# Unread products in TensorE's waits, counts taken out of a comparison, and another order of the first stages: a two-layer graph network on one core

## Chip, cores and metric

One core of a Trainium2 chip. The metric is the device time of one execution in microseconds (us). A core has five engines with a queue each: TensorE (PE: matrix products; PEld is its weight load), VectorE (DVE), ScalarE (ACT), GpSimd (POOL) and SyncE (SP, which here issues nearly all DMA transfers). A queue runs in order; engines wait for each other through semaphores.

## What is computed

There are 128 graphs of 128 nodes with 512 features. Both layers work on each graph alone:

```python
def hypergraph_conv(x, adj, W, b):
    H = (adj != 0).astype(x.dtype)
    w = adj.reshape(N, -1)[:, :C]                 # first row of adj
    xw = jnp.einsum('ncd,hd->nch', x, W)
    Dn = jnp.einsum('nce,ne->nc', H, w)
    Dn = jnp.where(Dn > 0, 1.0 / Dn, 0.0)
    Be = H.sum(axis=1)
    Be = jnp.where(Be > 0, 1.0 / Be, 0.0)
    m = Be[:, :, None] * jnp.einsum('nce,nch->neh', H, xw)
    out = Dn[:, :, None] * jnp.einsum('nce,neh->nch', H, m)
    return out + b
# layer 0
h = jnp.maximum(_layernorm(x), 0.0)
x0 = h
h = jax.nn.relu(hypergraph_conv(h, adj, W1, b1))  # 512 -> 1024
h = layer_norm(h, gamma, beta)
x = x + hypergraph_conv(h, adj, W2, b2) + x0      # 1024 -> 512
# layer 1
h = jnp.maximum(_layernorm(x), 0.0)
agg = (adj @ h) / jnp.maximum(adj.sum(-1), EPS)
x = x + jax.nn.relu(jnp.concatenate([h, agg], -1) @ W.T)
```

`Be` is one over the number of nodes in each hyperedge: the counts of the change.

## The kernel before

One graph fills the 128 partitions. A graph g passes through some sixty small stages (each a Python function that issues a few instructions), and five graphs are in flight. `step(s)` writes out by hand in which order the stages of graphs s-4 to s+2 are issued; there is a `head()` for the start, 131 calls of `step` (the stages that `head` or an index rule out are skipped), and a `tail()` for the last five graphs, called a to e (123 to 127). Nothing is reordered afterwards: the order of the calls is the order of each engine's queue, and semaphores are placed by data.

Weight products are split into high, low and difference parts: `product` (L376) runs the h and the l part of each into one bank of PSUM (rm, gm, bm, am by layer), and the d part into another (rd, gd, bd, ad), as fp32r products of 512 columns, four at a time: 0.9 us for four. Plain fp32 products are ps_s (L305, incidence matrix), pz (L343, features times node matrix), py (L517) and pc (L185, the beta row). Every split costs work on three engines: ACT writes h (L126 for weights, L356, L466), VectorE or POOL the l part, VectorE the d part.

What graph g needs, in the names of the trace: x is loaded (`load_x`), `x_sums`, `x_spread`, `scales`, `x_norm` make h0; `load_adjb` brings adj in blocks; `incidence` (L286, seven VectorE instructions) transposes it, sets it to 0 and 1, counts, and makes sb; `node_matrix` multiplies to ps_s and ACT copies it to s; `node_scale` makes dinv; `conv1_nodes` makes pz, which `conv1_high/low/rest` split into z; `conv1_weights` is rm and rd; `conv1_main`, `conv1_out`, `conv1_bias` make r; `inner_sums`, `inner_spread`, `inner_norm` normalise it; `inner_out` sends it to DRAM and `inner_in` reads it back in blocks (nb), `inner_turn` transposes (nt), `inner_high/low/rest` split it into nh, nl, nd; `conv2_weights` is gm and gd; g gets a bias (`conv2_bias`, c0) and goes into py; `conv2_out` adds py to x; `layer1_*` do the same normalising and trip for the second layer (h, hb, ht, hh, hl, hd) with products bm, bd (mean part) and am, ad (self part); `mean_*` make the mean operator from adj (`mean_operator` is four VectorE instructions, `mean_out` and `mean_in` a trip through DRAM); `aggregate` (L599) joins both; `finish` stores.

In the head the weights also come in and are split: `w1[half]`, `w2[half]` and `w3[half]` have `high(i)` on ACT, `low(i)` and `rest(i)` on VectorE, each for half of the columns; `scale_w2(k)` multiplies the second weights by gamma in place after `beta_row(k)` has read them on TensorE.

SP issues in program order and a DMA waits there for its buffers: `load_adjb` has two (`adjb`, L214), freed by the transpose in `incidence`. PSUM has eight banks: six named "w" (`bank`, L82) and two named "n" (`small_bank`, L86) for ps_s, pz and py.

Of the kernel before, what the change touches and what calls it, by code (L numbers as in the profile page):

```python
# [24 lines left out]
def gnn_kernel(  # L25
# [31 lines left out]
    nc = tc.nc  # L57
# [17 lines left out]
    def combine(eng, dst, a, b, op):  # L75

        width = 256 if eng is nc.gpsimd else dst.shape[1]
        for c in range(0, dst.shape[1], width):
            s = slice(c, c + width)
            eng.tensor_tensor(dst[:, s], a[:, s], b[:, s], op)  # L80

    def bank(name):  # L82

        return psum.tile([P, 512], FP, tag="w", name=name)

    def small_bank(name):  # L86

        return psum.tile([P, 512], FP, tag="n", name=name, bufs=2)

    done = set()  # L90

# [193 lines left out]
    @stage  # L285
    def incidence(g):  # L286


        HT[g] = at = pool.tile([P, P], FP, tag="ht", name="adjt")
        nc.vector.transpose(at, ADJB.pop(g))  # L290
        SB[g] = sb = pool.tile([P, P + 1], FP, tag="sb", name="sb")
        nc.vector.tensor_scalar(sb[:, P : P + 1], at[:, 0:1], DOWN_12, None, MUL)
        nc.vector.tensor_scalar(at, at, 0.0, None, ALU.not_equal)
        cnt = pool.tile([P, 1], FP, tag="cnt", name="cnt", bufs=2)
        nc.vector.tensor_reduce(cnt, at, AX.X, ADD)

        nc.vector.tensor_scalar(cnt, cnt, 1.0, None, MAX)
        nc.vector.reciprocal(cnt, cnt)
        nc.vector.tensor_scalar(sb[:, :P], at, cnt, None, MUL)
# [26 lines left out]
    @stage  # L326
    def x_spread(g):
        spread((1, g), X[g], H0[g], D)
# [47 lines left out]
    def product(left, halves, main, name):  # L376
        kk = KD * len(halves)

        def right(m, k):
            return getattr(halves[k // KD], "hld"[m])[:, k % KD, :]  # L380

        pm, pd = bank(name + "m"), bank(name + "d")
        for i in range(2):
            for k in range(kk):
                nc.tensor.matmul(pm, left[i](k), right(i, k), start=(i == 0 and k == 0),  # L385
                                 stop=(i == 1 and k == kk - 1))
        main(pm)
        for k in range(kk):
            nc.tensor.matmul(pd, left[2](k), right(2, k), start=(k == 0),  # L389
                             stop=(k == kk - 1), skip_group_check=True)  # L390
        return pd
# [291 lines left out]
    def head():  # L683
        copy(eps_root, eps, AF.Sqrt)
        load_x(0)
        load_adjb(2)
        for half in range(2):
            for i in range(2):
                load_w1(half, i)
        load_affine()  # L690
        load_adjb(0, nc.scalar)
        load_x(1)
        load_adjb(1)
        x_sums(0)
        load_adj(0)
        x_spread(0)
        for half in range(2):
            load_w2(half)
        load_bias(b2_bc, b2)
        w1[0].high(0)  # L700
        scales(0, 1)
        x_norm(0)
        w1[0].high(1)
        incidence(0)
        load_x(2)
        w1[0].low(0)
        node_matrix(0)
        conv1_nodes(0)
        w1[0].low(1)
        w1[1].high(0)  # L710
        w1[0].rest(0)
        conv1_high(0)
        w1[1].high(1)
        load_bias(b1_bc, b1)
        conv1_low(0)
        conv1_rest(0)
        incidence(1)
        x_sums(1, "A")
        x_spread(1)
        node_scale(0)  # L720
        w1[0].rest(1)
        scales(1, 1)
        w1[1].low(1)
        x_norm(1)
        conv1_weights(0, 0)
        beta_row(0)
        scale_w2(0, nc.scalar)
        conv1_main(0, 0)
        beta_row(1)
        scale_w2(1, nc.scalar)  # L730
        w1[1].low(0)
        w1[1].rest(0)
        w1[1].rest(1)
        node_matrix(1)
        node_scale(1)
        conv1_nodes(1)
        conv1_high(1, True)
        conv1_weights(0, 1)
        conv1_low(1)
        conv1_rest(1)  # L740
        beta_row(2)
        beta_row(3)
        conv1_main(0, 1)
        conv1_weights(1, 0)
        conv1_out(0, 0)
        scale_w2(2, nc.vector)
        scale_w2(3, nc.vector)
        conv1_bias(0, 0, nc.vector)
        w2[0].high(0)
        w2[0].high(1)  # L750
        conv1_out(0, 1)
        conv1_bias(0, 1, nc.vector)
        beta_row(4)
        beta_row(5)
        load_adjb(3)
        load_w3(0)
        load_w3(1)
        beta_row(6)
        beta_row(7)
        inner_sums(0)  # L760
        conv1_weights(1, 1)
        inner_spread(0)
        w2[0].low(1)
        residual(0)
        scale_w2(4, nc.vector)
        scale_w2(5, nc.vector)
        scales(0, 2)
        inner_norm(0)
        scale_w2(6, nc.vector)
        scale_w2(7, nc.vector)  # L770
        w2[0].low(0)
        incidence(2)
        inner_out(0)
        x_sums(2)
        x_spread(2)
        scales(2, 1)
        w2[1].high(0)
        w2[1].low(0)
        x_norm(2)
        node_matrix(2)  # L780
        w2[1].high(1)
        node_scale(2)
        load_adjb(4)
        conv1_nodes(2)
        conv1_main(1, 0)
        conv1_main(1, 1)
        conv1_high(2)
        w2[0].rest(1)
        conv1_low(2)
        conv1_rest(2)  # L790
        beta_out()
        inner_in(0)
        load_x(3)
        inner_turn(0)
        residual(1)
        conv1_out(1, 0)
        w3[0].high(0)
        conv1_bias(1, 0, nc.vector)
        w2[1].low(1)
        load_x(4)  # L800
        inner_high(0)
        conv1_weights(2, 0)
        conv1_out(1, 1)
        conv1_bias(1, 1, nc.vector)
        conv1_weights(2, 1)
# [8 lines left out]
        load_adjb(5)  # L814
        inner_rest(0)
        w3[0].high(1)
        w2[1].rest(1)
        incidence(3)
        conv2_weights(0)
        x_sums(3)  # L820
        x_spread(3)
        node_matrix(3)
        scales(3, 1)
        x_norm(3)
        residual(2)
        node_scale(3)
        conv2_main(0)
        conv1_main(2, 0)
        conv2_weights_out(0)
        conv1_nodes(3)  # L830
        conv2_bias(0, nc.vector)
        conv2_nodes(0)
        conv1_high(3, True)
        conv1_main(2, 1)
        conv1_low(3)
# [12 lines left out]
        scales(0, 3)  # L848
        inner_low(1, nc.vector)
        inner_rest(1)  # L850
        layer1_norm(0)
        layer1_trip_out(0)
        w3[1].high(0)
        conv2_weights(1)
        inner_sums(2)
        inner_spread(2)
        w3[0].low(1)
        scales(2, 2)
        conv2_main(1)
        inner_norm(2)  # L860
        conv2_weights_out(1)
        mean_operator(0)
        conv2_bias(1, nc.vector)
        inner_out(2)
        conv2_nodes(1)
        conv1_weights(3, 1)
        w3[1].low(0)
        mean_out(0)
        w3[0].low(0)
        conv2_out(1)  # L870
        layer1_trip_in(0)
        w3[1].high(1)
        mean_in(0)
        load_adj(1)
        x_sums(4)
        residual(3)
        x_spread(4)
        scales(4, 1)
        x_norm(4)
        incidence(4)  # L880
        layer1_turn(0)
        w3[1].low(1)
        layer1_high(0)
        node_matrix(4)
        mean_transpose(0)
        node_scale(4)
        layer1_low(0, nc.vector)
        inner_in(2)
        w3[0].rest(1)
        w3[1].rest(1)  # L890
        w3[1].rest(0)
        w3[0].rest(0)
        load_x(5)
        layer1_rest(0)
        load_adjb(6)

    def tail():
# [58 lines left out]
        layer1_low(c)  # L956
        finish(b)
        mean_out(c)
        conv2_nodes(d)
        layer1_rest(c)  # L960
        mean_in(c)
# [30 lines left out]
        mean_in(d)  # L992
        conv2_bias(e)
        finish(c)
        conv2_nodes(e)
        conv2_out(e)
        layer1_high(d)
# [82 lines left out]
```

## Time and profile before

| | |
|---|---|
| Time, median of 7 runs | 2514.29 us (2513.45 to 2516.66) |
| The profiled execution: time, span | 2513.88 us, 2512.1 us |
| Granted TensorE clock, mean of the span | 0.995 |
| Busy: PE, DVE, ACT, POOL | 2469.0, 2121.7, 1976.2, 1739.9 us |
| One graph in the body | 19.05 us |
| First product after which TensorE has no gap | 98.7 us |

How to read the profile: a line of instructions gives line, engine, operation, the tile written and the tiles read, the shape, and the count; a bracket names how long the engine sat idle before and whose work ended the wait. A fp32 product appears as two records. "Clock" is the share of TensorE's full clock that was granted in that stretch; TensorE's ends are modelled, so a product's row may overlap the next. A stretch is given by its limits in us from the start of the span.

### The profile page before, as it was taken

The numbers are of one execution on the slowest core, as the hardware profiler recorded it, in microseconds if no ns is written. First come the engines' busy times: TensorE is split into PE (matmuls) and PEld (weight loads), VectorE is DVE, ScalarE is ACT, GpSimd is POOL, SyncE is SP. The second block draws the span as 40 slices with busy tenths as digits, with TensorE's granted clock in tenths as the row PEclk, the third lists the DMA queues.
The fourth block names the chain that finished last, engine by engine and source line by source line (L and its number), as shares of the span: only waits on it lengthen the run. The fifth ranks groups of instructions, "written<-read, shape, count | busy, mean of one in ns | idle before, by whom it ended". The sixth has DMA issues, their size and how long they took to land.

```text
span 2512.1 us, 41377 instructions
## 1 busy us (share of the span) xinstructions
PE 2469.0 (98%) x11152; PEld 2003.6 (80%) x11152; DVE 2121.7 (84%) x4907; ACT 1976.2 (79%) x4112; POOL 1739.9 (69%) x2290
## 2 busy tenths in 40 slices
PE   6899999999999999999999999999999999999997
PEld 4688888888888888888888888888888888888885
DVE  7988888888888888888888888888888888888885
ACT  6787878788788888878878887887888778778874
POOL 2476777677677767767766776777677677677763
PEclk9999999999999999999999999999999999999998
DMA  6343444444344344434334443433443444344332
GB/s 175 102 121 121 128 125 124 126 127 123 121 129 126 119 126 128 123 124 131 120 119 127 128 124 123 131 121 123 126 128 121 126 128 123 120 127 128 120 120 83
DMA packets 409674, 311.90 MB, mean 124 GB/s; under 512 B 176736, under 2 KB 340576, under 8 KB 409440
## 3 DMA queue, kind: packets, MB, share of 16 engines
q1 hardware_dynamic: 408608, 309.18, 40.0%
q8 instruction: 88, 1.44, 0.2%
q14 instruction: 146, 1.20, 0.2%
q10 hardware_dynamic: 576, 0.07, 0.0%
q0 software_dynamic: 256, 0.01, 0.0%
HBM read 166.47 MB, written 142.61 MB: 123 GB/s over the span
## 4 chain that ended last, share of the span: by engine, by line
PE 94%; DVE 2%; DMA 1%; POOL 1%; issue 1%; ACT 1%; SPq 0%; POOLq 0%; DVEq 0%; ACTq 0%
PE rm L385 18%; PE gm L385 18%; PE bm L385 9%; PE am L385 9%; PE gd L389 9%; PE rd L389 9%; PE bd L389 5%; PE ad L389 4%; PE pz L343 4%; PE py L517 4%; PE am L599 2%; PE ad L599 1%; PE ps_s L305 1%; DMA adjb<-in_adj_dram 0%; POOL nl L80 0%
## 5 line engine op out<-in xcount | busy, mean ns | idle before, releaser
L80 POOL TENSOR_TENSOR g<-g,c 128x256 f32<-128x256 f32 x252 | 180.5, 737 | 524.2 <-DVE g L508 415.0
L80 POOL TENSOR_TENSOR r<-r,b_bc 128x256 f32<-128x256 f32 x500 | 356.2, 743 | 20.1 <-DVE st L234 11.1
L80 POOL TENSOR_TENSOR nl<-nt,nh 128x256 fp32r<-128x256 f32 x504 | 357.7, 743 | 5.0 <-ACT nh L466 5.0
L80 POOL TENSOR_TENSOR hl<-ht,hh 128x256 fp32r<-128x256 f32 x254 | 180.2, 731 | 146.2 <-ACT hh L466 146.2
L80 POOL TENSOR_TENSOR x_t<-x_t,h 128x256 f32<-128x256 f32 x256 | 240.2, 960 | 44.9 <-ACT h L239 44.9
L80 POOL TENSOR_TENSOR bl<-gb_t,bh 128x256 fp32r<-128x256 f32 x256 | 261.6, 1044 | 10.6 <-ACT anp L273 5.5
L504 ACT ACTIVATE g<-gm 128x512 f32<-128x512 f32 x128 | 76.5, 598 | 213.9 <-PE gm L385 213.9
L239 ACT ACTIVATE h<-x_t,st 128x512 f32<-128x512 f32 x256 | 207.7, 811 | 35.2 <-DVE st L235 27.0
L475 DVE SCALAR_TENSOR_TENSOR nd<-nh,nl 128x1024 fp32r<-128x1024 f32 x128 | 207.6, 1622 | 19.4 <-POOL nl L80 19.3
L445 DVE STREAM_TRANSPOSE nt<-nb 128x1024 f32<-128x1024 f32 x128 | 159.4, 1245 | 62.6 <-DMA nb<-n_scratch 61.7
L223 ACT ACTIVATE h<-x_t 128x512 f32<-128x512 f32 x256 | 160.2, 626 | 61.3 <-DVE x_t L521 59.3
L80 POOL TENSOR_TENSOR x_t<-x_t,b_bc 128x256 f32<-128x256 f32 x256 | 185.0, 742 | 14.2 <-DMA b_bc<-in_b_dram 14.2
L385 PE MATMUL rm<-w11h,z 128*128 128x512 f32 x512 | 191.1, 495 | 0.0
L228 ACT ACTIVATE h<-x_t,st 128x512 f32<-128x512 f32 x256 | 184.4, 720 | 4.3
L409 DVE SCALAR_TENSOR_TENSOR r<-rd,dinv,r 128x512 f32<-128x512 f32 x256 | 186.2, 727 | 0.8 <-ACT r L404 0.2
L404 ACT ACTIVATE r<-rm,dinv 128x512 f32<-128x512 f32 x256 | 171.2, 669 | 2.1 <-PE rm L385 1.2
L239 ACT ACTIVATE r<-r,st 128x1024 f32<-128x1024 f32 x128 | 158.2, 1236 | 1.3 <-DVE st L235 1.3
L385 PEld LDWEIGHTS rm<-w11h,z 128*128 128x128 f32 x512 | 97.2, 190 | 72.3 <-issue 60.3
L385 PE MATMUL bm<-w30h,hh 128*128 128x512 f32 x512 | 150.9, 417 | 3.3 <-ACT hh L466 3.3
L466 ACT ACTIVATE nh<-nt 128x1024 fp32r<-128x1024 f32 x128 | 135.2, 1056 | 18.4 <-DVE nt L445 17.8
L343 PEld LDWEIGHTS pz<-s,h 128*128 128x128 f32 x1024 | 134.3, 192 | 14.8 <-ACT s L307 4.0
L228 ACT ACTIVATE junk<-r,st 128x1024 bf16<-128x1024 f32 x128 | 145.2, 1134 | 0.1
(127 smaller groups left out, 7190.7 us busy)
## 6 DMA issues: line engine op xcount, KB each, us to landing
n_scratch<-r SPq DMA_DIRECT2D x128, 512.0 KB, 2.6
nb<-n_scratch SPq DMA_DIRECT2D x512, 128.0 KB, 2.8
x_t<-in_x_dram SPq DMA_DIRECT2D x128, 256.0 KB, 2.8
h_scratch<-h SPq DMA_DIRECT2D x128, 256.0 KB, 2.1
hb<-h_scratch SPq DMA_DIRECT2D x512, 64.0 KB, 2.0
out_dram<-o SPq DMA_DIRECT2D x128, 256.0 KB, 2.8
adj_t<-in_adj_dram SPq DMA_DIRECT2D x128, 64.0 KB, 1.8
an_scratch<-adj_t SPq DMA_DIRECT2D x128, 64.0 KB, 2.6
```

What stands on the lines that cost most here:

```text
L80: eng.tensor_tensor(dst[:, s], a[:, s], b[:, s], op)
L223: copy(junk, src, func, accum_out=t[:, 0:1])
L228: copy(junk, src, AF.Square, bias=t[:, 1:2], accum_out=t[:, 2:3])
L239: copy(dst, src, func, bias=t[:, 5:6], scale=t[:, 4:5])
L343: nc.tensor.matmul(z[:, k * P : (k + 1) * P], H0[g][:, k * P : (k + 1) * P], S[g], start=True, stop=True)
L385: nc.tensor.matmul(pm, left[i](k), right(i, k), start=(i == 0 and k == 0), stop=(i == 1 and k == kk - 1))
L389: nc.tensor.matmul(pd, left[2](k), right(2, k), start=(k == 0), stop=(k == kk - 1), skip_group_check=True)
L404: copy(R[g][:, HALVES[half]], PY.pop((g, half)), AF.Copy, scale=DN[g][:, 1:2])
L409: nc.vector.scalar_tensor_tensor(r, PR.pop((g, half)), dn[:, 0:1], r, MUL, ADD)
L445: nc.vector.transpose(nt.rearrange("p k (i b) -> p k i b", b=B), t.rearrange("p i k a -> p k i a"))
L466: copy(h, a, AF.Copy, scale=DOWN)
L475: nc.vector.scalar_tensor_tensor(t, h, 2.0**-12, low, MUL, SUB)
```

## The change

Three edits. A `fill(n)` notes a number of columns; the next PSUM bank that is handed out first receives plain fp32 products of that many columns (at most 512 each) of one constant column, `eps`, with itself, into the bank that the real product then overwrites. Thirteen such calls stand in `head` and `tail`; a second list, FILL_DIFF, stays empty. In `incidence` the comparison sums its own output. In `head` stages are moved.

```diff
+    FILL, FILL_DIFF = [], []
+    def fill(columns, diff=False):
+        (FILL_DIFF if diff else FILL).append(columns)
+    def filled(t, todo):
+        while todo:
+            columns = todo.pop()
+            while columns > 0:
+                w = min(columns, 512)
+                nc.tensor.matmul(t[:, :w], eps.to_broadcast([P, P]), eps.to_broadcast([P, w]),
+                                 start=True, stop=True, skip_group_check=True)
+                columns -= w
+        return t
     def bank(name):
-        return psum.tile([P, 512], FP, tag="w", name=name)
+        return filled(psum.tile([P, 512], FP, tag="w", name=name), FILL)
     def small_bank(name):
-        return psum.tile([P, 512], FP, tag="n", name=name, bufs=2)
+        return filled(psum.tile([P, 512], FP, tag="n", name=name, bufs=2), FILL)
@@ incidence
-        nc.vector.tensor_scalar(at, at, 0.0, None, ALU.not_equal)
         cnt = pool.tile([P, 1], FP, tag="cnt", name="cnt", bufs=2)
-        nc.vector.tensor_reduce(cnt, at, AX.X, ADD)
+        nc.vector.tensor_scalar(at, at, 0.0, None, ALU.not_equal, ADD, accum_out=cnt)
@@ head
         load_adjb(0, nc.scalar)
+        load_adjb(1)
         load_x(1)
-        load_adjb(1)
...
+        scales(0, 1)
...
         w1[0].high(0)
-        scales(0, 1)
+        load_x(2)
+        w1[0].high(1)
         x_norm(0)
-        w1[0].high(1)
         incidence(0)
-        load_x(2)
         w1[0].low(0)
+        fill(3072)
         node_matrix(0)
...
         conv1_rest(0)
-        incidence(1)
         x_sums(1, "A")
...
         x_norm(1)
+        fill(512)
+        incidence(1)
         conv1_weights(0, 0)
+        conv1_main(0, 0)
         beta_row(0)
         scale_w2(0, nc.scalar)
-        conv1_main(0, 0)
+        node_matrix(1)
         beta_row(1)
+        w1[1].low(0)
         scale_w2(1, nc.scalar)
-        w1[1].low(0)
         w1[1].rest(0)
         w1[1].rest(1)
-        node_matrix(1)
-        node_scale(1)
         conv1_nodes(1)
...
-        load_w3(0)
-        load_w3(1)
+        load_w3(1)
+        load_w3(0)
...
+        node_scale(1)
+        residual(0)
         beta_row(7)
         inner_sums(0)
...
         scale_w2(6, nc.vector)
+        x_sums(2)
         scale_w2(7, nc.vector)
         w2[0].low(0)
         incidence(2)
+        inner_norm(0)
+        fill(256)
         inner_out(0)
-        x_sums(2)
         x_spread(2)
         scales(2, 1)
         w2[1].high(0)
         w2[1].low(0)
+        node_matrix(2)
         x_norm(2)
-        node_matrix(2)
+        node_scale(2)
         w2[1].high(1)
-        node_scale(2)
         load_adjb(4)
+        fill(384)
         conv1_nodes(2)
...
         w3[0].high(0)
-        conv1_bias(1, 0, nc.vector)
+        fill(512)
+        load_x(3)
+        conv1_out(1, 1)
         w2[1].low(1)
         load_x(4)
+        conv1_bias(1, 0, nc.vector)
         inner_high(0)
         conv1_weights(2, 0)
-        conv1_out(1, 1)
...
         x_spread(3)
+        fill(256)
         node_matrix(3)
...
         conv2_weights_out(0)
+        fill(384)
         conv1_nodes(3)
         conv2_bias(0, nc.vector)
+        fill(256)
         conv2_nodes(0)
...
         conv2_weights(1)
+        layer1_trip_out(0)
+        mean_operator(0)
         inner_sums(2)
...
         conv2_weights_out(1)
-        mean_operator(0)
         conv2_bias(1, nc.vector)
         inner_out(2)
+        mean_out(0)
+        w3[1].low(0)
+        fill(1024)
         conv2_nodes(1)
...
-        conv2_out(1)
         layer1_trip_in(0)
...
         incidence(4)
+        conv2_out(1)
         layer1_turn(0)
         w3[1].low(1)
         layer1_high(0)
+        fill(384)
         node_matrix(4)
         mean_transpose(0)
         node_scale(4)
+        inner_in(2)
+        w3[0].rest(0)
         layer1_low(0, nc.vector)
-        inner_in(2)
         w3[0].rest(1)
+        layer1_rest(0)
+        w3[1].rest(0)
         w3[1].rest(1)
-        w3[1].rest(0)
-        w3[0].rest(0)
         load_x(5)
-        layer1_rest(0)
@@ tail
         mean_out(c)
+        fill(768)
         conv2_nodes(d)
...
         finish(c)
+        fill(768)
         conv2_nodes(e)
...
         layer1_rest(e)
+        fill(1536)
         layer1_mean(e)
```

In each engine's queue this leaves POOL's order as it was, moves two loads on SP (x of graph 1 behind the blocks of adj of graph 1; the halves of w3 exchanged), and changes the orders of TensorE, VectorE and ACT in the head as the diff says. The body and the tail keep theirs, but for the fills and the counts.

More of the change, by code (lines that the diff above doesn't have):

```diff
@@ L387, in product @@
         main(pm)
+        filled(pd, FILL_DIFF)
         for k in range(kk):
@@ L743, in head @@
         conv1_main(0, 1)
-        conv1_weights(1, 0)
+        w2[0].high(0)
         conv1_out(0, 0)
         scale_w2(2, nc.vector)
+        load_adjb(3)
         scale_w2(3, nc.vector)
+        conv1_weights(1, 0)
         conv1_bias(0, 0, nc.vector)
-        w2[0].high(0)
         w2[0].high(1)
@@ L753, in head @@
         beta_row(4)
+        load_w3(1)
+        load_w3(0)
         beta_row(5)
-        load_adjb(3)
-        load_w3(0)
-        load_w3(1)
         beta_row(6)
+        node_scale(1)
+        residual(0)
         beta_row(7)
@@ L761, in head @@
         conv1_weights(1, 1)
+        w2[0].low(1)
         inner_spread(0)
-        w2[0].low(1)
-        residual(0)
         scale_w2(4, nc.vector)
@@ L767, in head @@
         scales(0, 2)
-        inner_norm(0)
         scale_w2(6, nc.vector)
+        x_sums(2)
         scale_w2(7, nc.vector)
@@ L792, in head @@
         inner_in(0)
-        load_x(3)
         inner_turn(0)
@@ L813, in head @@
         inner_out(1)
-        load_adjb(5)
         inner_rest(0)
         w3[0].high(1)
+        load_adjb(5)
         w2[1].rest(1)
@@ L829, in head @@
         conv2_weights_out(0)
+        fill(384)
         conv1_nodes(3)
         conv2_bias(0, nc.vector)
+        fill(256)
         conv2_nodes(0)
         conv1_high(3, True)
+        conv1_low(3)
         conv1_main(2, 1)
-        conv1_low(3)
         conv1_rest(3)
@@ L851, in head @@
         layer1_norm(0)
-        layer1_trip_out(0)
         w3[1].high(0)
         conv2_weights(1)
+        layer1_trip_out(0)
+        mean_operator(0)
         inner_sums(2)
@@ L861, in head @@
         conv2_weights_out(1)
-        mean_operator(0)
         conv2_bias(1, nc.vector)
         inner_out(2)
+        mean_out(0)
+        w3[1].low(0)
+        fill(1024)
         conv2_nodes(1)
+        w3[0].low(0)
         conv1_weights(3, 1)
-        w3[1].low(0)
-        mean_out(0)
-        w3[0].low(0)
-        conv2_out(1)
         layer1_trip_in(0)
@@ L874, in head @@
         load_adj(1)
+        residual(3)
         x_sums(4)
-        residual(3)
         x_spread(4)
```

## The prediction

> **What bounds the kernel now.** I read the page first, then stretches of the span, the waits of TensorE, and its timeline at both ends.
>
> ```profile
> span 2512.1 us, 41377 instructions
> ...
> PEclk9999999999999999999999999999999999999998
> ```
>
> The profiled execution took 2513.88 us, 1.8 us more than its span; the median of the seven runs shown is 2514.29, 0.4 above it. My sum is made against 2513.88. What a measurement of this kernel can tell from no change is about 0.2%, 5.0 us. Three regimes show in the stretches (columns: busy us of PE, PEld, DVE, ACT, POOL, then the granted clock):
>
> ```profile
> 80.00:100.00 20.00, 15.32 (x61) 11.65 (x62) 19.34 (x38) 13.17 (x29) 10.14 (x12) 0.91 0.27 74
> 100.00:120.00 20.00, 20.00 (x92) 16.34 (x92) 17.54 (x40) 15.80 (x34) 13.95 (x20) 1.00 0.42 132
> ...
> 2490.00:2500.00 10.00, 5.25 (x18) 3.73 (x17) 4.94 (x13) 2.17 (x4) 2.83 (x4) 0.76 0.25 85
> ```
>
> From 98.7 us TensorE has no gap, at full clock, to about 2460: 19.05 us for each graph (rm L385 starts at 119.28, 138.34, 157.38 in the chain). Before that VectorE is the fullest (19.34 of 20). After 2460 nobody is full: one graph goes through transposes, splits, DMA trips and products in turn.
>
> ```profile
> PE ps_s L305 <- DVE sb L299: 11.8, 3, 9.9
> PE bd L389 <- DVE hd L475: 3.9, 1, 3.9
> ```
>
> Of the first 100 us TensorE waits 28, most of it for VectorE. The waits have a second price, the granted clock. Stretches of about 3.41 us, PE alone (busy, clock, DMA share, GB/s):
>
> ```profile
> 37.63:41.04 3.41, 1.65 (x10) 0.99 0.53 141
> 41.04:44.45 3.41, 2.14 (x5) 0.50 0.79 199
> 44.45:47.87 3.42, 3.42 (x9) 0.51 0.10 37
> 54.70:58.10 3.40, 2.04 (x9) 1.00 0.50 173
> 71.70:75.10 3.40, 0.97 (x4) 1.00 0.38 153
> 75.13:78.54 3.41, 3.41 (x9) 0.50 0.42 111
> 2481.50:2484.90 3.40, 1.69 (x5) 1.00 0.27 70
> 2484.94:2488.35 3.41, 3.41 (x9) 0.50 0.38 111
> ```
>
> A stretch with 0.97, 1.65 or 1.69 us busy is followed by half clock; one with 2.04 is not. Half clock ends after a full stretch (3.42), not after 2.14. So the bound lies between 1.69 and 2.04 busy of 3.41. Half clock doubles a product:
>
> ```profile
> 13.79 2.07 PE L385 MATMUL rm<-w10h,z 128*128 128x512 f32 x4 [0.69 <-ACT z L356]
> ...
> 51.38 1.07 PE L385 MATMUL gm<-w21h,nh 128*128 128x512 f32 x4
> ...
> 2483.55 1.13 PE L517 MATMUL py<-g,s 128*128 128x512 f32 x2 [1.62 <-POOL g L80]
> ...
> 2497.80 2.07 PE L385 MATMUL bm<-w30h,hh 128*128 128x512 f32 x4 [3.25 <-ACT hh L466]
> ```
>
> The first row says that the clock was half until about 17 us, though no clock value is recorded there.
>
> **The change, part by part.** *Price of a fill.* It is a plain fp32 product like py L517, which holds TensorE 0.86 us for 512 columns in the chain: 1.68 ns a column, 3.36 at half clock. 3072 columns take 5.2 us (10.3 at half), 1024 1.7, 768 1.3, 1536 2.6. All thirteen, 10,112 columns, are 17 us. Each stands in TensorE's order just before a product that waited, so it costs nothing as far as it is shorter than the wait.
>
> *Tail* (d is graph 126, e 127). The fill of 768 columns before py(d) lies in a wait of 1.77, the next in one of 1.62: both end before g arrives, price 0. The second brings its stretch from 1.69 to about 3.0 busy, so bm(d), at 2484.77, runs at full clock: 1.84 instead of 3.66. What follows: hd (2486.9) now releases bd; bd and am end at 2489.7 instead of 2491.2; the wait of POOL's bl L80 for am ends with them; the h trip of e, queued on SP behind bl (2492.78), goes 1.5 us earlier, and so does everything to bm(e). bm(e) waits 3.25 now; 2.6 of fill fit. At full clock bm(e) ends 1.9 earlier, but hd(e), 2.15 after its start, holds bd: bd at half clock took 1.2, then 0.9; to the end of am 2.5 is saved. The reload of the mean operator (issued to 2501.6, read at 2503.47) shifts by the first 1.5 only and becomes late next: it leaves 1.6. Tail: 1.5 + 1.6 = 3.1. If the second fill meets half clock it takes 5.2, 1.9 too long, and gives the second gain back: 1.2 is the low end.
>
> [...]
>
> *Head, start.* The fill of 3072 starts when eps is set (0.9) and ends between 6.1 and 11.2; sb(0) comes at 9.8, some 0.4 earlier with h(0) behind the second w10h, since POOL's x+h (9.01) then no longer slows L299 (0.75 against its usual 0.28). The clock should be open from then on. That speeds pz and rm (0.9 and about 2 us of the rows from 11 to 17), but these are covered:
>
> ```profile
> 8.09 0.23 DVE L293 TENSOR_SCALAR adjt<-adjt 128x128 f32<-128x128 f32 x1
> 8.35 0.29 DVE L295 TENSOR_REDUCE cnt<-adjt 128x1 f32<-128x128 f32 x1
> 8.67 0.15 DVE L297 TENSOR_SCALAR cnt<-cnt 128x1 f32<-128x1 f32 x1
> ...
> 17.35 1.22 DVE L136 TENSOR_TENSOR w10d<-w10l,w10h 128x1024 fp32r<-128x1024 f32 x1
> ...
> 71.33 0.16 DVE L234 RECIPROCAL st<-st 128x1 f32<-128x1 f32 x1 [1.18 <-ACT st L229]
> ```
>
> rd(0,0) waits for the second w10d (ends 18.5). The new order takes incidence(1), 1.8 us (15.01 to 16.79), from in front of it: about 16.4. The weights of beta_row(0) (issued to 14.4, 4.4 to landing) and incidence(1), now behind half of w11l, come next: 16.4 + 0.35 + 1.14 + 1.6 = 19.5 for sb(1). Then ps_s 0.25, pc 0.86 beside the copy s, pz 0.9, rm and rd(0,1) 2.7: 24.3 against 26.2 now. But TensorE waits some 2 of the 3.4 us before 19.5, and no fill stands there: half clock for a stretch takes up to 1.7 back. I take 1.2, bounds 0.2 and 1.9.
>
> SP: load_x(1) now stands behind load_adjb(1), whose buffer is free only after the transpose of incidence(0) (7.9), so x(1) is issued near 9.9 instead of 6.21. x_sums(1) reads it at about 13.9; 3.5 us to landing leaves 0.5, 5.2 (as adj_t) would cost 1.2, which the bound 0.2 takes in. adjb(3) waits for the transpose of incidence(1), now near 18; it was issued at 19.13. w31r before w30r: first read at 42, free. POOL keeps its order.
>
> *Head, middle.* x_sums(2) moves into ACT's 0.42 idle before inner_norm(0): all behind it up to z(2) comes 0.4 earlier; the trip of r, issued 0.55 later, lands about 43.6, when VectorE reaches nt. The fills of 256, 384 and 512 (0.4, 0.6, 0.9) fit in 1.21, 1.00, 1.42 and raise the 1.65 to some 2.8. That spares rm(2) 2.8 us at half clock, but not the path: gd waits for nd (53.98), the end of a full VectorE queue from 44.1. Carried: 0.4.
>
> *Counts.* L293 and L295 take 0.26 + 0.32 start to start. No row shows the merged operation. At best it costs what L293 does: 0.32 saved; if it writes the sum by a second small record, as ACT's sums do (0.19), 0.13; if it ran as slowly as both, 0. I take 0.13, nearest to ACT's row. Four of them lie on VectorE's full stretch: 0.5 (0 to 1.3). In the body they are worth nothing while TensorE is full (VectorE 17.5 of 20).
>
> *Head, end.* mean_operator(0), 0.9 us, moves from before g(1)'s bias into VectorE's 1.18 wait at 70.2. py(1) could start at 73.4 instead of 74.33; the fill of 1024 ends at 73.6. rm(3,1) then runs at full clock, 1.7 less. But sb(4) waits for st, which ACT ends at 75.93, and ht, hd and nt(2) follow in one full VectorE queue: ht at 78.6 for 79.04 now. Moving hd before w31d frees bd 2.4 earlier, and gm(2) then waits for nt(2). Carried: 0.4 (0 to 0.9).
>
> Head: 1.2 + 0.4 + 0.5 + 0.4 = 2.5. With the tail 5.6: 2513.9 - 5.6 = 2508.3; the low and high sums of the bounds are 2506.3 and 2512.1.
>
> **Rivals.** *The head gives nothing.* TensorE's time is spared but VectorE's queue keeps its end; the clock falls at 17 to 20 where no fill stands. For it: 19.34 of 20. Against: the moves shorten that queue. The tail alone: 2510.8.
>
> *More is carried.* Half clock costs TensorE some 8.7 us of the head (2.5 before 17, then 2.8, 1.7, 1.7). If reordering lets 4 us more of this through, 2504. For it: gd at 54.11 stands right behind nd and gm, both near the bound. Against: the full VectorE queue.
>
> *Slower: the fills don't open the clock.* Their operands are one constant column read over and over; no row shows such a product. If they ran at half clock and left it there, the first would end at 11.2 (+1.8), 1024 columns would take 3.4 in 1.5 (+1.9), 768 twice 2.6 in 1.7 (+1.8), 1536 5.2 in 3.25 (+1.9): 7.4, less some 3 that VectorE's queue and the moves cover: 2518. It decides from the point where a fill takes over 0.9 us for 512 columns after 8 us.
>
> **How the numbers follow.** Forecast 0.60, own range 2506 to 2511; nothing from the head 0.16; more carried 0.14; slower 0.10. Faster by over 0.2%: 0.55 of the first, 0.02 of the second, all 0.14 of the third: 0.71. Within 0.2%: 0.05 + 0.14 = 0.19. Slower: 0.10. Range 2503.5 to 2512.5: it leaves out the slower case and a little beyond the third.
>
> **What would show it.** Fills near 0.86 us for 512 columns from 8 us on; clock 1.00 at 41 to 48 and after 2484; first gapless product about 2.5 us before 98.7; one or two VectorE records in place of L293 and L295; bm(d) and bm(e) at 3.7 us or less together, where they take 7.4 now. Wrong: a fill that ends after its product's input, above all before bm(e), or a gate that closes in the body.

## The result and the profile after

The changed kernel takes 2508.67 us (median of 15 runs, 2507.36 to 2510.76) where the kernel before, on the same chip, takes 2514.65 (35 runs, 2513.45 to 2517.63): a ratio of 0.9975, 95% interval 0.9968 to 0.9982, or 6.0 us less. The forecast was 2508.3. The profiled execution took 2508.7 us. From the page of the changed kernel:

```profile
span 2506.9 us, 41470 instructions
...
PEclk9999999999999999999999999999999999999999
```

Stretches of the changed kernel, in the columns of those shown of before (busy us of PE, PEld, DVE, ACT, POOL, then clock, DMA share, GB/s):

```profile
80.00:100.00 20.00, 16.44 (x65) 10.99 (x64) 19.31 (x37) 13.71 (x30) 9.44 (x12) 1.00 0.24 77
100.00:120.00 20.00, 20.00 (x92) 16.17 (x91) 16.39 (x42) 15.77 (x33) 14.74 (x19) 1.00 0.40 122
2490.00:2500.00 10.00, 9.16 (x32) 5.73 (x32) 3.89 (x8) 2.69 (x5) 1.91 (x3) 1.00 0.23 66
...
8.50:11.91 3.41, 0.84 (x5) 0.65 (x6) 3.24 (x9) 3.05 (x5) 0.48 (x1) 1.00 0.95 325
11.91:15.32 3.41, 3.41 (x12) 2.24 (x11) 3.19 (x5) 2.48 (x4) 2.50 (x2) 0.50 0.92 255
```

VectorE is as full at 80 to 100 as it was (19.31 against 19.34), and the clock at 2490 rose from 0.76 to 1.00. Once the clock has opened, one half stretch is left ahead of the last product, at 11.9. Before had five (41.0 and 44.4, 75.1, 88.8 in the head, 2484.9 in the tail) and two more under bm(e). Two of TensorE's waits in the first 105 us of the changed kernel (us in total, times, the longest):

```profile
PE ps_s L321 <- DVE sb L315: 2.4, 2, 1.5
PE pc L202 <- DMA w20r<-in_w2t_dram: 1.1, 1, 1.1
```

The wait for sb is 2.4 us where it was 11.8: unread products now stand in it. A new wait, of the beta row for its weights, has appeared. The timeline of the changed kernel (start, busy, then as in the rows shown of before):

```profile
0.93 7.48 PE L94 MATMUL ps_s<-eps 128*128 128x512 f32 x12 [0.93 <-DVE eps L126]
...
54.26 0.29 DVE L311 TENSOR_SCALAR_CACHE_REDUCE adjt<-adjt 128x128 f32<-128x128 f32 x1
54.47 0.08 DVE L311 DVE_READ_ACCUMULATOR adjt<-adjt 128x1 f32 x1
54.59 0.15 DVE L313 TENSOR_SCALAR cnt<-cnt 128x1 f32<-128x1 f32 x1
...
2482.27 1.19 PE L401 MATMUL bm<-w30h,hh 128*128 128x512 f32 x4
...
2490.69 2.75 PE L94 MATMUL bm<-eps 128*128 128x512 f32 x6
2494.12 1.19 PE L401 MATMUL bm<-w30h,hh 128*128 128x512 f32 x4 [0.69 <-ACT hh L483]
...
2499.42 0.31 DVE L287 STREAM_TRANSPOSE ant<-anb 128x128 f32<-128x128 f32 x1 [1.06 <-DMA anb<-an_scratch]
```

1536 unread columns took 2.75 us and left 0.69 of the wait before bm(e), which ran at full clock: 1.19 where before shows 2.07. The merged count is two records, 0.33 from its start to the next instruction, where the two old ones took 0.58 (8.09 to 8.67 in the rows shown of before). The first 3072 columns took 7.48 us, at half clock to about 5.1 (the first clock record, 1.00, begins there): these products of one constant column do open the clock.

I cut the span where TensorE becomes and stops being full: "head" is the start of the first rm product of graph 4, "body" from there to the first rm of graph 127, "tail" from there to the end of the span. Before: 100.06, 2346.69, 65.34. After: 97.55, 2347.08, 62.26. The head gave 2.51 (forecast 2.5), the tail 3.08 (forecast 3.1), the body took 0.39 back.

### The profile page after: what moved, and what is told of

Read it like the earlier page. It is cut to its first block, busy times and chain, and to the rows that moved or that the text cites. A ratio compares the mean times of both kernels' runs of the same rounds, so it can differ in the third digit from the quotient of the medians.

```text
span 2506.9 us, 41470 instructions
## 1 busy us (share of the span) xinstructions
PE 2480.5 (99%) x11198; PEld 2003.5 (80%) x11198; DVE 2089.5 (83%) x4907; ACT 1977.0 (79%) x4112; POOL 1755.0 (70%) x2290
## 3 DMA queue, kind: packets, MB, share of 16 engines
q8 instruction: 88, 1.44, 0.2%
## 4 chain that ended last, share of the span: by engine, by line
PE 90%; POOL 3%; issue 2%; DVE 2%; DMA 1%; ACT 1%; SPq 0%; POOLq 0%; DVEq 0%; ACTq 0%
PE rm L401 17%; PE gm L401 17%; PE bm L401 9%; PE gd L406 9%; PE rd L406 9%; PE am L401 9%; PE bd L406 4%; PE pz L359 4%; PE ad L406 4%; PE py L534 4%; PE am L616 2%; PE ad L616 1%; PE ps_s L321 1%; POOL nl L80 1%; POOL r L80 1%
## 5 line engine op out<-in xcount | busy, mean ns | idle before, releaser
L80 POOL TENSOR_TENSOR bl<-gb_t,bh 128x256 fp32r<-128x256 f32 x256 | 275.3, 1098 | 7.9 <-PE am L401 7.9
L252 DVE TENSOR_TENSOR st<-st 128x1 f32<-128x1 f32 x384 | 136.0, 354 | 13.2
```

The costliest lines, as they stand in the source:

```text
L252: nc.vector.tensor_tensor(t[:, 5:6], t[:, 1:2], t[:, 4:5], MUL)
```

## The experiments

All were run with the kernel before on the same chip; chips differ by up to 4 us (medians of before 2512.46 to 2516.14), so times are given as a difference to that median and as a ratio with its interval. An interval is about 2 us to either side, as wide as most effects here; the cut of one trace is sharper, but each trace is one draw: the limits of the 3.41 us stretches, at which the clock changes, stand at another place of the span from trace to trace (divided by 3.4133 us they leave 0.04 in before and 3.36 in its second trace, 1.67 in the changed kernel and 1.99 in its second). A number in brackets behind a tile is its graph, as in rm(1) (for pc the block of the weights; rd(0,1) is graph 0, second half). The column "rm(1)" is the start of graph 1's first rm product.

| Kernel | rm(1) | head | body | tail | against before | ratio (95%) |
|---|---|---|---|---|---|---|
| before | 27.51 | 100.06 | 2346.69 | 65.34 | | |
| before, second trace | 30.20 | 103.18 | 2344.54 | 64.60 | | |
| order alone | 27.56 | 100.53 | 2346.05 | 64.34 | -0.3 | 0.9997 (0.9988 to 1.0005) |
| counts alone | 27.90 | 102.11 | 2344.40 | 65.15 | -2.3 | 0.9992 (0.9983 to 1.0001) |
| unread products alone | 28.37 | 100.91 | 2349.06 | 62.49 | -1.9 | 0.9991 (0.9982 to 1.0000) |
| order and counts | 26.28 | 98.53 | 2345.61 | 63.39 | -5.1 | 0.9978 (0.9969 to 0.9987) |
| the same, and the tail's three | 26.33 | 98.49 | 2344.69 | 63.11 | -7.0 | 0.9972 (0.9960 to 0.9983) |
| the same, and three of the head's | 26.78 | 98.20 | 2344.16 | 63.70 | -3.9 | 0.9986 (0.9977 to 0.9994) |
| changed, old counts | 26.64 | 98.34 | 2348.83 | 62.55 | -4.4 | 0.9983 (0.9974 to 0.9992) |
| changed | 26.26 | 97.55 | 2347.08 | 62.26 | -6.0 | 0.9975 (0.9968 to 0.9982) |
| changed, second trace | 29.70 | 100.12 | 2345.61 | 62.24 | -5.6 | 0.9976 (0.9966 to 0.9986) |
| changed, last one doubled | 28.45 | 99.24 | 2345.13 | 63.52 | -3.5 | 0.9985 (0.9976 to 0.9994) |
| changed, and 640 columns before pc(0) | 26.16 | 97.44 | 2344.56 | 62.52 | -6.1 | 0.9973 (0.9963 to 0.9984) |
| the same, second trace | 26.12 | 97.29 | 2345.66 | 62.42 | -4.8 | 0.9980 (0.9971 to 0.9989) |

**Without any unread product** (order and counts stay):

```diff
-        fill(3072)
...
-        fill(1536)
```

> The changed kernel with all thirteen fills taken out; the new order and the merged count stay. Theory of the forecast (the fills pay in the tail alone, because there TensorE's products at half clock stand on the path; in the head VectorE's queue ends last): the tail goes back to 65.3 us from the first product of graph 127 (62.3 in the changed kernel), the head gives back 0.5 at most, so the first product of graph 4 starts at 97.6 to 98.1 us and the time is 2508.7 + 3.1 + (0 to 0.5) = 2511.8 to 2512.3, with half clock near 41 and 75 us again. Rival (the head's gain comes from the clock, not from the order): the head goes back too, first product of graph 4 near 100 us, time 2514 or more.

Measured: head 98.53, tail 63.39. The head kept 1.5 of its 2.5, so most of it is not the clock's. The tail did not go back to 65.34: here bm(d) ran at full clock by itself and bm(e) alone met half clock.

**With the tail's three alone:**

```diff
-        fill(3072)
...
-        fill(384)
         node_matrix(4)
```

> The changed kernel with the ten fills of the head taken out and the three of the tail kept. Theory of the forecast: 2508.7 to 2509.2, tail 62.3 us, first product of graph 4 at 97.6 to 98.1 us though the clock is half for several us in the head. Rival (the clock makes the head's gain): tail 62.3 us, first product of graph 4 near 100 us, time 2511 or more.

Measured: head 98.49, the same again, tail 63.11. The place of the missing 0.95 shows in this kernel's stretches, and then in its timeline:

```profile
55.71:59.13 3.42, 1.26 (x10) 1.01 (x9) 2.46 (x9) 3.08 (x7) 2.05 (x3) 1.00 0.57 154
59.13:62.54 3.41, 3.41 (x6) 2.09 (x7) 2.44 (x4) 0.85 (x3) 1.18 (x2) 0.50 0.03 9
```

```profile
59.09 2.07 PE L534 MATMUL py<-g,s 128*128 128x512 f32 x2 [0.88 <-DVE g L80]
...
61.20 0.75 DVE L538 SCALAR_TENSOR_TENSOR x_t<-py,dinv,x_t 128x512 f32<-128x512 f32 x1 [0.97 <-PE py L534]
```

After 1.26 us busy the clock halves, py(0) takes 2.07 us for 1.13, and VectorE, whose next instruction reads it, waits 0.97. In the changed kernel that wait does not exist: x_t starts at 60.28, and everything after it is 0.9 earlier. Of the six traces without unread products at this place, five met half clock at py(0) and VectorE waited 0.72 to 0.97 us; none of the eight with them did. The one that was spared is before's first, so this 0.95 is no part of the 2.51 between the first traces. The tail, 0.85 longer than the changed kernel's, lost that ahead of py(e); from there to the last product both take 20.72 us. The half stretches at 38.6 and 42.1 in the same run cost nothing: nd(0) starts at 51.43, at 51.46 in the changed kernel.

**Unread products alone** (old order, old counts):

```diff
+        fill(3072)
         node_matrix(0)
...
+        fill(1536)
         layer1_mean(e)
```

> The kernel before with the thirteen fills put before the same stages, and nothing else: old order, old counts. Theory of the forecast: the tail gains 3.1, the head 0 to 0.6, so 2514.65 - 3.1 - (0 to 0.6) = 2511.0 to 2511.6; the clock is full in the head from about 15 us and TensorE waits longer for VectorE instead. Rival (the clock makes the head's gain): the head gains most of 2.5 too, near 2509.2. If fills overshoot their waits in the old order, over 2512.

Measured: head 100.91, tail 62.49. The tail's part is here whole; in the head nothing came. rm(1) is 0.9 later than in before's first trace, 0.47 of it a wait of VectorE for graph 1's adj blocks at 15.9; from rm(1) to graph 4 it takes 72.54, before took 72.55.

**Old counts:**

```diff
+        nc.vector.tensor_scalar(at, at, 0.0, None, ALU.not_equal)
         cnt = pool.tile([P, 1], FP, tag="cnt", name="cnt", bufs=2)
-        nc.vector.tensor_scalar(at, at, 0.0, None, ALU.not_equal, ADD, accum_out=cnt)
+        nc.vector.tensor_reduce(cnt, at, AX.X, ADD)
```

> The changed kernel with the comparison and the sum as two operations again. The trace of the changed kernel shows 0.33 us from the start of the merged one to the next instruction where the two took 0.58: 0.25 saved each. Theory (the counts pay where VectorE's queue ends last: graphs 2 to 5, perhaps 1): the head loses 4 x 0.25 = 1.0, the body nothing, time 2509.4 to 2509.9. Rival (the counts are covered in the head as well): 2508.7, the same as the changed kernel. Other rival (the shorter VectorE queue also pays in the body): 2510 or more.

Measured: head 98.34, 0.79 later than with the merged count, 0.41 of it behind rm(1); no half clock in the head of either after 17 us.

**The kernel before, once more:**

> The kernel before, unchanged, for a second trace of it. Theory: the stretches of about 3.41 us, after which the clock may fall, run on freely, so their limits stand at another place of the span than in the first trace (there the limits are at 41.04 plus or minus multiples of 3.4133 us), and which products of the tail meet half clock changes with them: tail (first rm of graph 127 to the end of the span) anywhere from 63.3 to 65.4 us, head (first rm of graph 4) 99.9 to 101.0, a graph 19.06 us. Rival (the first trace stands for every run): head 100.06 and tail 65.34, each within 0.15.

Measured: head 103.18, tail 64.60, time 2514.11. The head is 3.1 later, more than the whole gain between the first traces. It is also later than expected. By rm(1) 2.7 of it are lost: VectorE waited 0.44 for z and 0.30 for adj blocks, TensorE came to the beta row at 20.75 instead of 19.19, and the clock opened at 23.8 instead of 17.1, so that the pc products there took 3.42 us where they had taken 1.95.

**The order alone:**

```diff
+        nc.vector.tensor_scalar(at, at, 0.0, None, ALU.not_equal)
-        nc.vector.tensor_scalar(at, at, 0.0, None, ALU.not_equal, ADD, accum_out=cnt)
+        nc.vector.tensor_reduce(cnt, at, AX.X, ADD)
...
-        fill(3072)
```

> The kernel before with the new order of the head alone: no unread products, counts in two instructions. Theory: the head's gain is the order's (about 0.8 us), the counts' (0.8) and the three unread products' ahead of py(0) (0.95): here the first rm of graph 4 starts at 99.2 to 99.5 where before has 100.1 to 100.9, and the tail stays at 63.3 to 65.4; 0.5 to 1.5 us below before, so no difference that a whole time can tell. Rival (the order only made room for the counts and the unread products, and is worth nothing alone): head 100.0 or more. Rival (the order is worth all of the 1.5 that were left without unread products): head 98.5.

Measured: head 100.53; 0.3 us below before in time, an interval that holds no more than 3. The theory's 99.2 to 99.5 failed in this trace: pc(0) waited 0.55 for w20r until 20.39 (19.12 in the kernel with order and counts), and a half stretch at 60.7 made VectorE wait 0.97 for py(0), as above.

**Three of the head's:**

```diff
         x_spread(3)
         fill(256)
         node_matrix(3)
...
         fill(384)
         conv1_nodes(3)
...
         fill(256)
         conv2_nodes(0)
```

> The changed kernel with three of the thirteen unread products: 256 columns before ps_s(3), 384 before pz(3), 256 before py(0); the other ten and all of the tail's are out. Theory: these three alone carry what the head's unread products are worth, because py(0) and its copy into x stand in VectorE's queue right behind z(3): at half clock py(0) takes 1.1 us instead of 0.55 and VectorE waits 0.97 for it. Then the first rm of graph 4 starts at 97.5 to 97.8 (98.5 without any, 97.55 with all), no half clock between 55 and 65 us, tail 63.3 to 65.4. Rival (the gain comes from the first 3072 columns or from the 1024 before py(1)): 98.4 to 98.6.

Measured: head 98.20, between the two forecasts, but from an rm(1) 0.5 later. From rm(1) to graph 4 it takes 71.42, as the changed kernel does (71.29); without any it takes 72.25 and 72.16. No half clock lies between 45.0 and 79.1. In these traces the three carry what the head's unread products are worth behind rm(1), 0.8. On whole times nothing of it shows: three of the head's give 3.9 below before and none 5.1, the tail's three alone 7.0 and all thirteen 6.0 and 5.6, each known to some 2 us.

**The last one doubled:**

```diff
-        fill(1536)
+        fill(3072)
```

> The changed kernel with the last unread product doubled, 3072 columns instead of 1536 before bm(127). They take 5.2 us from 2490.7 where the wait is 3.4, so bm(127) starts 1.7 late. Theory: hd covers the first 0.5 of it (bd waits for hd until 0.4 us after bm ends), the rest is carried: tail 1.2 longer, 63.3 to 63.7 where the changed kernel has 62.3 to 62.6. Rival (VectorE and POOL set the end there): under 0.3 longer. Rival (all of it is carried): 1.7 longer, 64.0 to 64.3.

```profile
2490.47 5.34 PE L94 MATMUL bm<-eps 128*128 128x512 f32 x12
2495.24 1.48 PE L401 MATMUL bm<-w30h,hh 128*128 128x512 f32 x4
```

These lines of its timeline show bm(e) right behind the unread products, with no wait for hh left. They took 4.8 us, not 5.2; this run is 0.18 ahead of the changed kernel's at py(e), so bm(e) is 1.3 late against 2494.12. The tail is 63.52, 1.26 longer: the number that the theory gave, but not its split. The excess is 1.3, and hardly anything of it is covered. The surprise is the head, 99.24, though nothing there was changed: half clock at 20.5 to 24.0.

**The counts alone:**

```diff
-        nc.vector.tensor_scalar(at, at, 0.0, None, ALU.not_equal)
         cnt = pool.tile([P, 1], FP, tag="cnt", name="cnt", bufs=2)
-        nc.vector.tensor_reduce(cnt, at, AX.X, ADD)
+        nc.vector.tensor_scalar(at, at, 0.0, None, ALU.not_equal, ADD, accum_out=cnt)
```

> The kernel before with the merged count alone: old order, no unread products. Theory: each count is 0.25 us shorter on VectorE (0.33 start to next instead of 0.58) and three of them lie on VectorE's full queue between the first rm of graph 1 and that of graph 4: this interval takes 71.9 to 72.3 us, where the three traces with old counts and no unread products have 72.55, 72.98 and 72.97. The time is 0.5 to 1.5 below before. Theory B (VectorE's queue also has slack of its own in the body that rare late transfers use up, so the shorter count saves TensorE waits there too): body (first rm of graph 4 to that of graph 127) at most 2345.5, where old counts had 2344.5 to 2349.1, and the time 2 to 3 us below. Rival (0.13 each as forecast, not 0.25): interval 72.2 to 72.6.

Measured: 74.21 from rm(1) to graph 4, outside both forecasts for it and 1.7 above before's first trace. Some 0.9 of that arises at py(0), which met half clock at 61.1, and 0.8 after 97 us, behind two half stretches (88.4 to 95.2) where before has one. The draw outweighs the counts. The body, 2344.40, is on the side of theory B, but before's second trace has 2344.54. Inconclusive, but for the 0.25 of each count on VectorE.

**The changed kernel, once more:**

> The changed kernel, unchanged, for a second trace. Theory: the limits of the 3.4133 us stretches stand elsewhere, the clock opens by 8 us (the first 3072 columns fill a whole stretch wherever it begins), one half stretch follows between 8 and 24 us, none between 25 us and the last product; first rm of graph 4 at 97.4 to 99.4, late only if the half stretch covers pc(0) and pz(1) (19 to 23 us); tail 62.2 to 62.6; interval from the first rm of graph 1 to that of graph 4 70.8 to 71.4. Rival (the first trace was a lucky one): a half stretch between 35 and 95 us or in the tail before 2500, and an interval over 71.8.

Its stretches, and then lines of its timeline:

```profile
15.65:19.06 3.41, 0.91 (x3) 0.30 (x2) 2.99 (x9) 2.33 (x5) 0.00 (x0) 1.00 1.06 223
19.06:22.48 3.42, 2.78 (x5) 1.61 (x6) 3.32 (x6) 0.69 (x2) 0.00 (x0) 0.50 1.07 217
22.48:25.89 3.41, 3.41 (x12) 2.45 (x11) 0.65 (x1) 1.17 (x4) 0.77 (x2) 0.50 1.06 317
```

```profile
19.70 2.05 PE L202 MATMUL pc<-w20r,gb 128*128 128x512 f32 x2 [2.54 <-DMA w20r<-in_w2t_dram]
...
23.68 1.92 PE L359 MATMUL pz<-s,h 128*128 128x128 f32 x8
...
26.26 0.69 DVE L376 TENSOR_TENSOR z<-pz,z 128x512 fp32r<-128x512 f32 x1 [3.13 <-ACT z L372]
```

Behind the wait for w20r (2.54, to 19.70 instead of 19.11) the clock halved for two stretches, pc took 2.05 us and pz(1) 1.92, where they take 1.09 and 1.16 at full clock, and VectorE stood 3.13 us. Head 100.12, 2.57 later than in the first trace. Two clauses of the theory failed: one half stretch between 8 and 24 us (there are two) and a head of 99.4 at most. Behind rm(1) it takes 70.42, 0.4 less than forecast, with no half clock ahead of the last product, and the tail is 62.24, as forecast. So the first trace of the changed kernel was a lucky draw at its start, and so was that of before (rm(1) at 27.51, in the second trace 30.20).

**640 columns more, before pc(0):**

```diff
+        fill(640)
         beta_row(0)
```

> The changed kernel with one unread product more: 640 columns into the bank of pc(0), before beta_row(0), 1.08 us at full clock in the wait for w20r (1.1 to 2.5 us long so far). Theory: TensorE waits 2.4 of the 3.41 us before pc(0); with the fill no stretch there has under 2.0 us busy, so half clock cannot fall on pc(0) and pz(1) as it did at 20.5 to 24.0 in the trace of the doubled product, where z(1) waited 1.61 for it. The first rm of graph 1 at 26.0 to 26.8, never 28 or more; everything behind as in the changed kernel; time 0 to 0.7 below it on the same chip, no difference that can be told. Rival (the fill outlasts the wait, since w20r lands sooner than it ends): first rm of graph 1 0.3 to 1 later and the time above the changed kernel's.

Measured: rm(1) 26.16, no half clock ahead of the last product, time 2507.46, with 2508.05 for the changed kernel on that chip: no difference that can be told.

> The kernel with 640 columns before pc(0), unchanged, for a second trace at another place of the stretches. Theory: no 3.41 us stretch between 8 and 95 us has under 1.8 us busy, wherever the limits stand, so no half clock lies on pc(0) and pz(1): first rm of graph 1 at 26.0 to 26.8, first rm of graph 4 at 97.3 to 98.2, tail 62.2 to 62.6. The time is 0.24 to 0.3% below before on the same chip. Rival (the trace before was a lucky one, as the first of the changed kernel was): a half stretch between 15 and 26 us and the first rm of graph 1 at 28 or more.

The second trace fell, by chance, almost on the draw of the changed kernel's second one (limits 0.09 us apart, modulo 3.413). Its stretches, and lines of its timeline:

```profile
12.15:15.56 3.41, 3.41 (x10) 2.15 (x9) 3.17 (x8) 2.77 (x7) 1.92 (x2) 0.50 0.91 261
15.56:18.97 3.41, 3.40 (x14) 2.34 (x14) 3.27 (x9) 2.35 (x5) 0.00 (x0) 1.00 1.04 225
```

```profile
17.72 1.24 PE L94 MATMUL pc<-eps 128*128 128x512 f32 x4
18.98 1.09 PE L202 MATMUL pc<-w20r,gb 128*128 128x512 f32 x2
```

The stretch that had 0.91 us busy has 3.40 (some of it rm and rd, which the half stretch at 12.15 pushed back, and 1.24 of unread product); pc(0) takes 1.09 for 2.05 and rm(1) starts at 26.12 for 29.70. One clause failed: a stretch under 1.8 busy did occur, at 8.7 (1.17), and the half stretch behind it is harmless, as the forecast says of that place. The time is 4.8 below before, 0.20% where the theory has 0.24 to 0.3, which the interval does not tell apart: on whole times this version stands level with the changed kernel. What it buys is a start that neither of its two traces lost; the changed kernel's start came 2.2 and 3.4 us later in two of the three traces it has (the doubled last product leaves its head as it was).

## Why the forecast held, step by step

The total held, and for the two executions first profiled so did both its parts. The runs show where that was luck.

**Start of the head, 1.2 (0.2 to 1.9).** Measured between the first traces: rd(0,1) from 25.29 to 24.03, 1.26. The new wait named there (weights of beta_row(0)) is the 1.1 in the list of waits. Order and counts together bring it, and not the early clock: the three kernels with both and with neither the 3072 columns nor the 512 have rm(1) at 26.28, 26.33 and 26.78. Neither alone shows a gain (27.56 and 27.90; before has 27.51 and 30.20), but w20r lands up to 1.4 us apart from trace to trace (18.85 to 20.26): with the order alone pc(0) came 1.27 later than with both, 0.55 of that a wait for w20r, and rm(1) came the same 1.27 later. So these traces do not say what each is worth alone. What was mis-sized is "half clock for a stretch takes up to 1.7 back". In the two traces in which it struck, rm(1) came 2.2 and 3.4 later; less the 0.7 and 0.6 by which w20r was late, 1.5 and 2.8. One stretch cost what the forecast says, but there can be two, because the first half one is not full either (2.78). An early clock is what lets it close: without the 3072 columns the clock opens at 17.7 to 18.7 in these three, behind rm and rd at half clock, and does not fall on pc. Opening the clock ahead of one wait, with nothing in the next, is worth nothing here, and can cost.

**Middle, 0.4: did not come.** nt(0) gained 1.14, no more than the start had. x_sums(2) did move into ACT's 0.42, but ACT then stood 0.39 for ps_s(2) at 37.60, and z(2) started 1.09 earlier. The failing step is "all behind it up to z(2) comes 0.4 earlier": it left out that VectorE, which makes sb(2), gains nothing from it.

**Counts, 4 times 0.13.** Each is 0.25 on VectorE: the sum's record of 0.08 is far shorter than ACT's 0.19, from which it was taken. VectorE's busy time does not confirm this size: it fell by 32.2 us between the first traces, which happens to be 128 times 0.25, but by 13.5 with the counts alone, and by 23 from the mean of the five traces with old counts to that of the nine with merged ones. With old counts the head came 0.79 later, in one trace of each.

**End, 0.4 (0 to 0.9): about 0.8.** From nt(1) to graph 4's rm the gain grew from 1.43 to 2.51; 0.25 of the 1.08 is the count of graph 4. The bias of g(1) went from 73.50 to 71.30 with the mean operator out of its way, and VectorE's wait there from 1.18 to 0.27; the forecast had "ht at 78.6", it started at 77.21. Without any unread product this part takes as long (35.24 us from nt(1) to graph 4's rm, 35.22 in the changed kernel, 36.30 before, one trace each), so the order and the count carry it, and not the 1024 columns.

**Tail, 3.1: 3.08 here, about 1.9 in the mean.** That the total fits is luck in this trace too. Rows of before, then of the changed kernel:

```profile
2484.77 1.95 PE L385 MATMUL bm<-w30h,hh 128*128 128x512 f32 x4
...
2491.95 0.39 PE L599 MATMUL am<-bh,anp 128*128 128x512 f32 x1
...
2504.41 1.08 PE L389 MATMUL ad<-w31d,hd 128*128 128x512 f32 x4
2505.32 0.39 PE L599 MATMUL am<-bh,anp 128*128 128x512 f32 x1
```

```profile
2488.28 0.39 PE L616 MATMUL am<-bh,anp 128*128 128x512 f32 x1
...
2499.21 1.07 PE L406 MATMUL ad<-w31d,hd 128*128 128x512 f32 x4
2500.13 0.49 PE L616 MATMUL am<-bh,anp 128*128 128x512 f32 x1
```

At bm(d) the full clock gave 1.17 and not 1.5: from bm(d) to the first product with the mean operator it was 7.18 us (2484.77 to 2491.95) and is 6.01 (2482.27 to 2488.28). Another 0.35 came ahead of py(e), at waits for nh and nd; there the traces lie up to 1.2 apart, with unread products in the tail or without. At bm(e) the forecast had 2.5 saved to the end of am, of which the late reload of the mean operator leaves 1.6. Measured, 1.52 is saved from bm(e) to ad (6.61 us, now 5.09), and the reload takes nothing back: VectorE does wait 1.06 for anb, but the product that reads the mean operator starts 0.92 behind ad, where it was 0.91. So the 2.5 was mis-sized, and the wait that was to cut it down is not on the path. The 0.69 left of bm(e)'s wait is as forecast.

The forecast was also made from one trace, in which both bm(d) and bm(e) met half clock. Six traces without tail products have 63.39 to 65.34, mean 64.4; the seven with them, the doubled one left out, 62.24 to 63.11, mean 62.5. From py(e) to the last product, which leaves the waits for nh and nd out, the seven take 20.65 to 20.86 us and the six 21.73 to 23.47: by the draw, the tail's unread products are worth 0.9 to 2.8 there, 1.8 in the mean.

**The rivals.** "The head gives nothing" fails on the cut. "More is carried" is not what these two traces show. "The fills don't open the clock" fails on the 5.1 us: had they been counted as idle, the first clock record would have come with the real products. Its price, however, a fill that outlasts its wait, was measured: 1.26 for 1.3.

**The granted clock.** In the kernel without unread products the clock halved at 59.66 after waits of only 1.28 and 0.88, behind a stretch with 1.44 us busy. That kernel's half stretches begin at 39.2, 59.7 and 2493.4, which are 6 and 713 times 3.4133 us apart. In before they begin at 41.00, 75.13, 88.78, 2484.94 and 2495.18: 10, 4, 702 and 3 times. So each of these traces keeps one set of limits from end to end, but the second trace of before, and that of the changed kernel, has another set than the first, and the program does not fix where they stand. This is what the forecast lacked: it took the limits of one trace as fixed, and so priced products which a half stretch hits by a draw.

**Still open.** Head and tail make about 4.5 of the 6 us in the mean (heads of before 100.06 and 103.18, of the changed kernel 97.55, 100.12 and 99.24; tails 1.9). Bodies with merged counts have 2344.2 to 2347.1 (nine traces, mean 2345.2), with old counts 2344.5 to 2349.1 (five, mean 2347.0). The forecast said that counts are worth nothing there; the ranges overlap, and this is not settled. Nor is the split between order and counts: together they are 5.1 below before, alone 0.3 and 2.3, each known to some 2 us.

## What to carry to other kernels

Read the granted clock from several executions: what one trace shows at half clock is a draw, and a product that stands ahead of the full queue should be kept from it whether or not it was hit. Filling one wait can open the clock just early enough to lose it in the next (rm(1) came 2.2 and 3.4 us later here), so fill each wait up to the real work, and each by less than its shortest length. When an idle slot on one engine is used up, look which other engine's result the next instruction needs before counting the slot as gained.

## What the hardware showed unexpectedly

Between 25 and 2499 us, over all fourteen traces, a stretch with up to 1.73 us busy of 3.41 could be followed by half clock and one with 1.63 or more could be left alone (1.70 from 2481.53 in before was followed by it; 1.64 from 2464.47 there and 1.74 from 76.76 in the changed kernel were not); every one under 1.63 was followed by it, none from 1.74 on. This is about half the stretch (1.71), but it is no sharp bound: ends of products are modelled, and at the end of the kernel without unread products a stretch with 1.93 us (2500.19 to 2503.61) was followed by half clock. Once half, the clock came back after every stretch with 3.04 us or more and after none with 2.86 or less (in before after 3.41 from 44.41, not after 2.10 from 41.00; in its second trace not after 2.84 from 61.39). The plain products of one constant column counted as busy time here: with no other product ahead of it the clock of the changed kernel opened at 5.1 us, and its stretch from 2489.99, with 3.24 us busy of which 2.7 are theirs, was followed by full clock. In the body, single graphs take 0.1 to 1.1 us longer than 19.06, in places that partly recur (the step from graph 87 to 88 in seven of the fourteen traces). The longest is the one from graph 23 to 24 of the changed kernel, 20.16: two blocks of nb landed 5.3 to 5.6 us after their issue, where the twelve of the three trips before took 2.6 to 2.9, VectorE waited 2.69 for them, and TensorE 0.26 for nd. One trace, the kernel with three of the head's unread products, has none, and the shortest body, 2344.16. What causes them was not tried.
